# Layer 0's router input: transposing six of eight batches with VectorE blocks and a DRAM round trip instead of TensorE

## The chip, the cores and the metric

The kernel runs on one core of a Trainium2 chip. The metric is the device time of one execution in microseconds. Before the change the median of three runs is 2222.36 us (2220.96 to 2223.24). The profile is of one execution more, which took 2228.55 us. Engines are named as the profile names them: PE is TensorE (PEld its weight loads), DVE is VectorE, ACT is ScalarE, POOL is GpSimd, and SP issues most DMA transfers.

## The reference

Input x has 8 batches of 512 tokens with 512 values, all float32. Four stages follow each other, each with a residual and a layernorm:

```python
x = _layernorm(x + _L0_attn_ref(x, ...))   # 16 causal heads of 32
x = _layernorm(x + _L0_ffn_ref(x, ...))    # 8 experts, top 2 per token
x = _layernorm(x + _L1_attn_ref(x, ...))   # 8 query heads of 64, 2 key/value heads
x = _layernorm(x + _L1_ffn_ref(x, ...))    # gated feed-forward, integer weights
```

Only the seam between the first two is touched. The router of the second stage takes the normalised rows of the first and needs, per token, 8 logits, a softmax and the two largest:

```python
router_logits = xf @ gate_weight.T + xf @ gate_delta.T
probs = jax.nn.softmax(router_logits.astype(jnp.float32), axis=-1)
routing_weights, selected = jax.lax.top_k(probs, TOP_K)
```

## The kernel before

The function `attention0` computes the first stage batch by batch (b = 0 to 7). A batch has four groups of four heads (g = 0 to 3), and a group has three units (u = 0 to 2), which split the causal scores by key tile: 512, 384 + 128 and 256 query columns wide. Below, (g, u) names a unit. In every unit TensorE computes the scores `sc` of the unit (L1356), then some extra work that the plan of the batch puts there, and then the product `av` of the unit before with the values (L1380). In unit u = 1 it also forms the row sums `rs` of the group before (`normalise`, L1395). ScalarE turns `sc` into `p` with an exponential (L1360), GpSimd masks `p` (L1365), and VectorE adds up the `p` of a group (L1388), inverts the row sums (L1398, 3.3 us each) and scales `av` into `aoT` (L1399).

The extra work comes from `plan(b)`, which maps each unit to a list of calls:

- `value`, `query`, `key` (L1282 to L1303) make the values of this batch and the queries and keys of the next group. Each is one set of four matmuls into one PSUM tile.
- `project(b-1, t)` (L1305) is the output projection of the batch before, one call for each of the four token tiles. The last one calls `layernorm` (L173), which normalises the rows on VectorE (L185) and stores them to DRAM (`rows`, L188).
- `turn(b-1, c)` (L1315) transposes the normalised rows with four TensorE transposes of 128 x 128 into one PSUM tile, copied to SBUF as `x1T` by VectorE (L194) or ScalarE (L192). Four calls, c = 0 to 3, make the whole `x1T`.
- `score(b-1)` (L1326) multiplies `x1T` with the router's weights into `ps_logits` (L491), copied out by ScalarE (L1330).
- `choose(b-1)` (L1332, L494) sums the logits' parts on TensorE (`ps_r`, L503) and then runs softmax and top 2 as some 26 small VectorE instructions with one ScalarE exponential (L512).
- `dispatch(b-2)` and `enter(b-2)` (L1335, L1345) rank the tokens per expert (`ps_rank`, L547) and enter them in a table: 24 one-hot rows on VectorE (L577 to L579), then 16 matmuls `ps_table` (L588).
- `merge` (L1404) adds one chunk of LoRA weights to each of two experts: two matmuls `ps_lora` into two PSUM tiles (L781), two scaled copies on ScalarE (L792), two additions on GpSimd (L794).

All these PSUM tiles (`ps_v`, `ps_q`, `ps_k`, `ps_o`, `rs`, `ps_x1T`, `ps_logits`, `ps_r`, `ps_rank`, `ps_table`, `ps_lora`) come from one pool with one tag and two buffers, `mm`, used in turn: a third tile waits until the first is copied out. `sc` has a single buffer. Every engine runs its own instructions in order, and the order inside the first seven batches is made by a scheduler from the order of the calls; from the third group of the last batch on it is the written order. SP's queue is one such order too: the `rows` stores (L188), the loads of `xT` (L1244) and of `x` (L1248) stand in it. GpSimd also adds a bias to each batch's `x` (L1474), which needs that load.

A way of transposing without TensorE is already in the kernel, in the class `Turn` (L73 to L102), which the third and the fourth stage use: VectorE transposes 32 x 32 blocks inside each 128 x 512 tile (`blocks`), four DMAs store the result to DRAM so that the blocks fall into their places (`out`, 256 KB each in pieces of 512 bytes), and one DMA of 1 MB loads it back (`back`). The columns of the result stand in another order, which `by_tile` undoes in a later copy:

```python
def blocks(self, room, t, x):
    out = room.rearrange("p (j t c) -> p j t c", t=self.n, c=32)[:, :, t, :]
    self.nc.vector.transpose(out, x.rearrange("p (j c) -> p j c", c=32))

def out(self, room):
    for i in range(self.N):
        src = room[32 * i : 32 * (i + 1), :].rearrange("r (k j f) -> r k j f", j=self.N, f=self.n * 32)
        self.nc.sync.dma_start(out=self.dram.rearrange("(j r) k i f -> r k j i f", j=self.N)[:, :, :, i, :], in_=src)

def back(self, room):
    self.nc.sync.dma_start(out=room, in_=self.dram.rearrange("p k i f -> p (k i f)"))
```

Of the kernel before, what the change touches and what calls it, by code (L numbers as in the profile page):

```python
# [9 lines left out]
F32 = mybir.dt.float32  # L10
# [3 lines left out]
AF = mybir.ActivationFunctionType  # L14
ALU = mybir.AluOpType
# [3 lines left out]
P = 128  # L19
NB = 8  # L20
S = 512
D = 512
NT = S // P
ND = D // P
# [29 lines left out]
V_BQ, V_BK, V_NS, V_SS, V_SG, V_SU = 0, 4, 8, 12, 16, 16 + NHID  # L54
# [18 lines left out]
class Turn:  # L73
# [11 lines left out]
# [4 lines that stand above are left out]
# [662 lines left out]
class Experts:  # L751
# [8 lines left out]
    def room(self, i):  # L760

        at = 4 * EXPERT + i * ND * 512
        return self.w[:, at : at + ND * 512].rearrange("p (u f) -> p u f", f=512)
# [450 lines left out]
def attention0(env, guard, keep, routes, experts, dram, p_mm, tiles_ctx):  # L1214
# [4 lines left out]
    tc, nc, ins, xs, vec = env.tc, env.nc, env.ins, env.xs, env.vec  # L1219
# [3 lines left out]
    with ExitStack() as phase:  # L1223
        work = phase.enter_context(tc.tile_pool(name="a_work", bufs=1))
# [54 lines left out]
        def mm(shape, name):  # L1279
            return p_mm.tile(shape, F32, tag="mm", name=name)  # L1280

        def value(b, t):  # L1282
            ps = mm([P, D], "ps_v")
            for c in range(ND):
                nc.tensor.matmul(ps, lhsT=xts[b][:, c, ts(t, P)], rhs=wv[:, c, :], start=c == 0, stop=c == ND - 1)  # L1285
            vs[t] = own.tile([P, D], F32, tag=f"v{t}", name=f"v{t}")
            nc.vector.tensor_tensor(vs[t], ps, row[:, 0, :], ALU.add)  # L1287

        def query(b, g):
            ps = mm([P, S], "ps_q")  # L1290
            for c in range(ND):
                nc.tensor.matmul(ps, lhsT=wq[:, g, ts(c, P)], rhs=xts[b][:, c, :], start=c == 0, stop=c == ND - 1)  # L1292
            q = own.tile([P, S], F32, tag="q", name="q", bufs=2)
            nc.vector.tensor_scalar(q, ps, vec[:, V_BQ + g : V_BQ + g + 1], None, ALU.add)
            heads[b, g] = [q]

        def key(b, g):
            ps = mm([P, S], "ps_k")
            for c in range(ND):
                nc.tensor.matmul(ps, lhsT=wk[:, g, ts(c, P)], rhs=xts[b][:, c, :], start=c == 0, stop=c == ND - 1)  # L1300
            k = own.tile([P, S], F32, tag="k", name="k", bufs=2)
            nc.scalar.activation(k, ps, AF.Identity, bias=vec[:, V_BK + g : V_BK + g + 1])
            heads[b, g].append(k)  # L1303

        def project(b, t):  # L1305
            ps = mm([P, D], "ps_o")
            for c in range(ND):
                nc.tensor.matmul(ps, lhsT=aoTs[b][:, c, ts(t, P)], rhs=wo[:, c, :], start=c == 0, stop=c == ND - 1)
            nc.vector.tensor_tensor(xs[b][:, t, :], ps, xs[b][:, t, :], ALU.add)
            if t == NT - 1:  # L1310
                env.layernorm(b, router.rows[S * b : S * (b + 1)])

        x1Ts, logits = {}, {}

        def turn(b, c):  # L1315
            if c == 0:
                x1Ts[b] = work.tile([P, ND, S], F32, tag="x1T", name="x1T")
            ps = mm([P, S], "ps_x1T")
            for t in range(NT):
                nc.tensor.transpose(ps[:, ts(t, P)], xs[b][:, t, ts(c, P)], env.ident)  # L1320
            if b == NB - 2:
                nc.scalar.copy(x1Ts[b][:, c, :], ps)
            else:
                env.evacuate(c, x1Ts[b][:, c, :], ps)

        def score(b):  # L1326
            ps = mm([P, S], "ps_logits")
            router.logits(x1Ts.pop(b), ps)
            logits[b] = work.tile([P, S], F32, tag="logits", name="logits")
            nc.scalar.copy(logits[b], ps)  # L1330

        def choose(b):  # L1332
            router.choose(b, logits.pop(b), mm([P, NT, E], "ps_r"))

        def dispatch(b):  # L1335
            router.dispatch(b, mm([P, NT, E], "ps_rank"))
# [3 lines left out]
        def one_hot(b, places):  # L1340
            if places[0] == 0:
                rooms[b] = work.tile([P, ND, S], F32, tag="x1T", name="one_hot")
            return router.one_hot(b, rooms[b], places)

        def enter(rows):  # L1345
            router.enter(mm([P, 2, E * E_TILES], "ps_table"), *rows)

        def scores(b, g, u):
            q, k = heads[b, g]
            sc = p_sc.tile([P, 4, S], F32, tag="sc", name="sc")  # L1350
            width = 0
            for kt in UNITS[u]:
                w = S - P * kt
                for j in range(4):
                    hs = slice(HD * j, HD * (j + 1))
                    nc.tensor.matmul(sc[:, j, width : width + w], lhsT=k[hs, ts(kt, P)], rhs=q[hs, P * kt :],  # L1356
                                     start=True, stop=True)
                width += w
            p = own.tile([P, 4, width], F32, tag=f"p{u}", name="p", bufs=2 if u == 0 else 1)
            nc.scalar.activation(p, sc[:, :, :width], AF.Exp, scale=scale)  # L1360

            at = 0
            for kt in UNITS[u]:
                first = p[:, :, at : at + P]
                nc.gpsimd.affine_select(out=first, in_=first, pattern=[[0, 4], [1, P]], compare_op=ALU.is_ge, fill=0.0,  # L1365
                                        base=0, channel_multiplier=-1)
                at += S - P * kt
            return p
# [41 lines left out]
        def plan(b):  # L1410

            todo = {(g, u): [] for g in range(ND) for u in range(len(UNITS))}
            for slot, places in (((0, 0), (0, 1)), ((0, 1), (3,)), ((0, 2), (2,))):
                todo[slot] += [lambda t=t: value(b, t) for t in places]
            for g in range(ND):
                nb, ng = (b, g + 1) if g + 1 < ND else (b + 1, 0)
                if nb < NB:
                    todo[g, 1].append(lambda nb=nb, ng=ng: query(nb, ng))
                    todo[g, 2].append(lambda nb=nb, ng=ng: key(nb, ng))
            pb, last = b - 1, b == NB - 1  # L1420
            if b:
                places = ((1, 0), (1, 0), (1, 1), (1, 1) if last else (1, 2))
                for t, slot in enumerate(places):
                    todo[slot].append(lambda t=t: project(pb, t))
                places = ((2, 0),) * 4 if last else ((2, 1), (2, 1), (2, 2), (2, 2))
                for c, slot in enumerate(places):
                    todo[slot].append(lambda c=c: turn(pb, c))
                todo[(2, 1) if last else (3, 0)].append(lambda: score(pb))
                todo[(2, 2) if last else (3, 1)].append(lambda: choose(pb))
                if not last:  # L1430
                    todo[2, 0].append(merge)
                    todo[3, 0].append(merge)
            if b == 0:
                todo[1, 0].append(lambda: router.merge_lora(mm([P, ND, E], "ps_wr")))
            if b > 1:
                todo[0, 2].append(lambda: dispatch(b - 2))
                todo[1, 1].append(lambda: enter(one_hot(b - 2, range(NT))))
            if last:
                todo[1, 2].append(soon)
                todo[2, 2].append(first_rows)  # L1440
                todo[3, 1].append(lambda: dispatch(b - 1))
                todo[3, 2].append(begin)
            return todo
# [17 lines left out]
        begun = phase.enter_context(ExitStack())  # L1461
        begun.enter_context(in_order(tc))
        query(0, 0)
        key(0, 0)
        order = phase.enter_context(ExitStack())
        waiting = summing = None
        for b in range(NB):
            todo = plan(b)
            for g in range(ND):
# [16 lines left out]
                for u in range(len(UNITS)):  # L1486
                    p = scores(b, g, u)
# [15 lines left out]
        b = NB - 1  # L1503
# [11 lines left out]
        for c in range(ND):  # L1515
            turn(b, c)
        tiles.step()
        score(b)
        merge()
        choose(b)  # L1520
# [651 lines left out]
```

## Time and profile before

| | us |
|---|---|
| median of three runs | 2222.36 |
| the profiled execution | 2228.55 |
| its span | 2226.8 |
| PE busy in the span | 2191.9 (98%) |
| DVE busy | 1273.7 (57%) |
| ACT busy | 632.0 (28%) |
| POOL busy | 487.6 (22%) |
| `ps_v` of batch 1 starts | 84.25 |
| `ps_v` of batch 7 starts | 644.44 |

The page gives busy times over the whole span, which has stages with different limits. The change lies in the first stage, up to about 745 us, so the views that matter are those of this stretch: the order in time of each engine, and the waits. Two things are to be kept in mind in reading them. The ends of matmuls are modelled, so a wait inside a group of matmuls can be counted as busy; the distance from one group's start to the next is the safer measure. And a group in the order of time is merged: `x4` are four instructions; a float32 matmul of the program shows as two instructions here, a transpose as one.

### The profile page before, as it was taken

To read this page: it belongs to the slowest core of one execution; us is meant where nothing else is said; L and a number is where in the kernel's file an instruction comes from. 1 tells how busy PE (TensorE), PEld (TensorE's weight loads), DVE (VectorE), ACT (ScalarE), POOL (GpSimd) and SP (SyncE) were. 2 spreads that over 40 slices of the span, in tenths; PEclk is the share of its full clock that TensorE was granted. 3 is DMA by queue.
4 is the path that set the end of the run, shared out by engine and by line. 5 is a ranking of instruction groups with operands and counts; after the bars stand their busy time and mean duration, and the time that the engine had idled before them with its cause. 6 is when DMAs were issued, how large, how long until landed. Compare 5 with 4: busy or idle time off the path is not lost. (4 is left out here: it accounts for less than half of the span.)

```text
span 2226.8 us, 23678 instructions
## 1 busy us (share of the span) xinstructions
PE 2191.9 (98%) x9006; PEld 1116.6 (50%) x9006; DVE 1273.7 (57%) x2032; ACT 632.0 (28%) x917; POOL 487.6 (22%) x489
## 2 busy tenths in 40 slices
PE   9999999999999999999999999999999999999997
PEld 3344444444444444444443333333343778888876
DVE  3556666666666633323316887798757655555443
ACT  2332323323233232122124333223332222222222
POOL 2322423234132333122105222222211000000000
PEclk9999999999999899999999999999999999999999
DMA  8010101101022216888735212312110321111000
GB/s 297 20 57 1 57 10 48 58 1 58 5 71 94 85 57 181 227 218 214 191 114 193 80 57 86 95 55 77 45 32 13 109 78 57 57 57 57 20 20 21
DMA packets 146428, 182.20 MB, mean 82 GB/s; under 512 B 60530, under 2 KB 89202, under 8 KB 144514
## 3 DMA queue, kind: packets, MB, share of 16 engines
q1 hardware_dynamic: 135024, 144.91, 21.0%
q0 software_dynamic: 10560, 34.61, 5.5%
q8 instruction: 74, 1.21, 0.2%
q10 hardware_dynamic: 722, 1.07, 0.1%
q14 instruction: 48, 0.39, 0.1%
HBM read 117.38 MB, written 63.18 MB: 81 GB/s over the span
## 5 line engine op out<-in xcount | busy, mean ns | idle before, releaser
L903 PE MATMUL ps_gu<-experts,xrT 128*128 128x512 f32 (+1 forms) x520 | 248.8, 601 | 0.0
L1360 ACT ACTIVATE p<-sc 128x2048 f32<-128x2048 f32 (+1 forms) x96 | 152.8, 1592 | 190.0 <-PE sc L1356 183.1
L1148 DVE SCALAR_TENSOR_TENSOR hT<-ps_u,vec,sg 128x512 f32<-128x512 f32 x88 | 65.6, 745 | 195.2 <-PE ps_u L1143 195.2
L1365 POOL TENSOR_SCALAR_AFFINE_SELECT p<-p 128x512 f32<-128x512 f32 x128 | 91.6, 729 | 385.2 <-ACT p L1360 378.5
L1159 PE MATMUL ps_f<-ffn_w,h_half 128*128 128x512 f32 x672 | 170.2, 394 | 0.6 <-issue 0.4
L998 POOL TENSOR_TENSOR g_total<-g_total,r_inv 128x512 f32<-128x512 f32 x64 | 89.7, 1401 | 358.3 <-DVE r_inv L1735 283.0
L1705 ACT ACTIVATE p<-sc 128x1024 f32<-128x1024 f32 x128 | 124.0, 1021 | 105.9 <-PE sc L1702 100.8
L1735 DVE RECIPROCAL r_inv<-r_inv 128x512 f32<-128x512 f32 x32 | 107.1, 3346 | 78.8 <-ACT r_inv L995 78.8
L1388 DVE TENSOR_TENSOR p<-p 128x1536 f32<-128x1536 f32 (+2 forms) x96 | 129.4, 1348 | 39.2 <-POOL p L1365 22.2
L905 DVE TENSOR_TENSOR h<-ps_gu,h 128x256 f32<-128x256 f32 x67 | 28.4, 424 | 212.8 <-ACT h L904 212.8
L903 PEld LDWEIGHTS ps_gu<-experts,xrT 128*128 128x128 f32 x520 | 96.2, 197 | 89.7 <-issue 89.5
L1159 PEld LDWEIGHTS ps_f<-ffn_w,h_half 128*128 128x128 f32 x672 | 124.4, 188 | 33.0 <-DVE h_half L1154 5.6
L1143 PE MATMUL ps_g<-x_high,ffn_w 128*128 128x512 f32 x352 | 138.9, 395 | 0.8 <-DVE x L1676 0.8
L1143 PE MATMUL ps_g<-x_low,ffn_w 128*128 128x512 f32 x352 | 139.1, 395 | 0.0
L1143 PE MATMUL ps_u<-x_low,ffn_w 128*128 128x512 f32 x352 | 138.8, 394 | 0.0
L1143 PE MATMUL ps_u<-x_high,ffn_w 128*128 128x512 f32 x352 | 138.7, 394 | 0.0
L919 PE MATMUL ps_y<-experts,hT 128*128 128x512 f32 (+1 forms) x272 | 127.9, 593 | 0.5 <-ACT hT L913 0.5
L1702 PE MATMUL sc<-qT,kT 64*128 64x512 f32 x512 | 127.3, 615 | 1.0 <-ACT qT L1609 0.7
L1292 PE MATMUL ps_q<-experts 128*128 128x512 f32 x256 | 121.1, 615 | 4.4 <-DMA experts<-in_xT 4.4
L1724 PE MATMUL av<-p,v 128*64 128x512 f32 x512 | 123.8, 605 | 0.0
L1285 PE MATMUL ps_v<-experts 128*128 128x512 f32 x256 | 118.0, 609 | 3.3 <-DVE v L1287 3.3
L1670 PE MATMUL ps_o<-attn_out,aoT 128*128 128x512 f32 x256 | 117.9, 605 | 0.8 <-ACT r_inv L995 0.8
(262 smaller groups left out, 3438.5 us busy)
## 6 DMA issues: line engine op xcount, KB each, us to landing
results<-y SPq DMA_DIRECT2D x68, 256.0 KB, 2.3
turned<-turned SPq DMA_DIRECT2D x56, 256.0 KB, 4.1
pair<-xrT SPq DMA_DIRECT2D x25, 512.0 KB, 3.4
xrT<-pair SPq DMA_DIRECT2D x100, 128.0 KB, 4.5
x<-in_x SPq DMA_DIRECT2D x8, 1024.0 KB, 7.5
experts<-in_gate_up SPq DMA_DIRECT2D x8, 1024.0 KB, 10.8
rows<-x SPq DMA_DIRECT2D x32, 256.0 KB, 2.0
x<-rows SPq DMA_DIRECT2D x8, 1024.0 KB, 15.5
```

What stands on the lines that cost most here:

```text
L903: nc.tensor.matmul(ps, lhsT=xT[:, c, :], rhs=self.weights(i, c), start=c == 0, stop=c == ND - 1)
L919: self.nc.tensor.matmul(ps, lhsT=hT[:, c, :], rhs=self.weights(i, ND + c), start=c == 0, stop=c == self.NI - 1)
L1143: nc.tensor.matmul(ps, lhsT=w[:, ts(dc, P)], rhs=x[:, dc, :], start=(dc, i) == (0, 0), stop=(dc, i) == (ND - 1, 1))
L1159: self.nc.tensor.matmul(os[t], lhsT=h[:, ts(t, P)], rhs=self.weights(2 * NHID + c), start=(c, i) == (0, 0), stop=(c, i) == (NHID - 1, 1))
L1285: nc.tensor.matmul(ps, lhsT=xts[b][:, c, ts(t, P)], rhs=wv[:, c, :], start=c == 0, stop=c == ND - 1)
L1292: nc.tensor.matmul(ps, lhsT=wq[:, g, ts(c, P)], rhs=xts[b][:, c, :], start=c == 0, stop=c == ND - 1)
L1360: nc.scalar.activation(p, sc[:, :, :width], AF.Exp, scale=scale)
L1388: nc.vector.tensor_tensor(total[:, :, P * kt :], total[:, :, P * kt :], p[:, :, at : at + w], ALU.add)
L1670: nc.tensor.matmul(ps, lhsT=state[b]["aoT"][:, c, ts(t, P)], rhs=w_out[:, c, :], start=c == 0, stop=c == ND - 1)
L1702: nc.tensor.matmul(sc[:, j, :], lhsT=st["kT"][hs, ts(kt, P)], rhs=st["qT"][g][hs, :], start=True, stop=True)
L1705: nc.scalar.activation(p, sc, AF.Exp, scale=scale)
L1724: nc.tensor.matmul(st["av"][HD * j : HD * (j + 1), :], lhsT=st["v"][:, kt, HD * j : HD * (j + 1)], rhs=p[:, j, :], start=kt == 0, stop=kt ...
```

## The change

For batches 0 to 5 (`by_blocks = NB - 2`) the transposes of `turn` are replaced by `blocks(b)`: four VectorE block transposes, four stores, one load, all through `Turn`. Batches 6 and 7 keep `turn`. `score` of these batches moves from the first unit of group 3 into its last, ahead of the key of the next batch, and its copy puts the columns in order; in the last batch it stays in (2, 1), but ahead of the query. `choose` moves into the next batch's first unit, `dispatch` from (0, 2) to (1, 0), and `enter` from (1, 1) to (1, 2). The four `project` calls are spread over four units. In batches 1 to 6 the two `merge` calls move from (2, 0) and (3, 0) to (2, 2) and (3, 1). The query of the next batch moves from (3, 1) to (3, 0). In batches 1 to 6 ScalarE copies out the query of group 3, which VectorE did before.

```diff
             q = own.tile([P, S], F32, tag="q", name="q", bufs=2)
-            nc.vector.tensor_scalar(q, ps, vec[:, V_BQ + g : V_BQ + g + 1], None, ALU.add)
+            if g == ND - 1 and 0 < b <= by_blocks:
+                nc.scalar.activation(q, ps, AF.Identity, bias=vec[:, V_BQ + g : V_BQ + g + 1])
+            else:
+                nc.vector.tensor_scalar(q, ps, vec[:, V_BQ + g : V_BQ + g + 1], None, ALU.add)
...
+        by_blocks = NB - 2
+        turns = Turn(env, dram, NT, "turned0")
+
+        def room(b):
+            x1Ts[b] = work.tile([P, ND, S], F32, tag="x1T", name="x1T")
+
+        def blocks(b):
+            room(b)
+            flat = x1Ts[b].rearrange("p k s -> p (k s)")
+            for t in range(NT):
+                turns.blocks(flat, t, xs[b][:, t, :])
+            turns.out(flat)
+            turns.back(flat)
+
         def turn(b, c):
             if c == 0:
-                x1Ts[b] = work.tile([P, ND, S], F32, tag="x1T", name="x1T")
+                room(b)
...
-            nc.scalar.copy(logits[b], ps)
+            if b < by_blocks:
+                nc.scalar.copy(turns.by_tile(logits[b], False), turns.by_tile(ps, True))
+            else:
+                nc.scalar.copy(logits[b], ps)
...
+            pb, last = b - 1, b == NB - 1
+            by_dma = 0 <= pb < by_blocks
             for g in range(ND):
                 nb, ng = (b, g + 1) if g + 1 < ND else (b + 1, 0)
                 if nb < NB:
-                    todo[g, 1].append(lambda nb=nb, ng=ng: query(nb, ng))
+                    todo[g, 0 if by_dma and ng == 0 else 1].append(lambda nb=nb, ng=ng: query(nb, ng))
                     todo[g, 2].append(lambda nb=nb, ng=ng: key(nb, ng))
-            pb, last = b - 1, b == NB - 1
             if b:
-                places = ((1, 0), (1, 0), (1, 1), (1, 1) if last else (1, 2))
+                places = ((1, 0), (1, 1), (1, 2), (2, 0)) if by_dma else ((1, 0), (1, 0), (1, 1), (1, 1) if last else (1, 2))
                 for t, slot in enumerate(places):
                     todo[slot].append(lambda t=t: project(pb, t))
-                places = ((2, 0),) * 4 if last else ((2, 1), (2, 1), (2, 2), (2, 2))
-                for c, slot in enumerate(places):
-                    todo[slot].append(lambda c=c: turn(pb, c))
-                todo[(2, 1) if last else (3, 0)].append(lambda: score(pb))
-                todo[(2, 2) if last else (3, 1)].append(lambda: choose(pb))
+                if by_dma:
+                    todo[2, 1].append(lambda: blocks(pb))
+                else:
+                    for c in range(ND):
+                        todo[2, 0].append(lambda c=c: turn(pb, c))
+                todo[(3, 2) if by_dma else (2, 1)].insert(0, lambda: score(pb))
+                if not by_dma:
+                    todo[2, 2].append(lambda: choose(pb))
                 if not last:
-                    todo[2, 0].append(merge)
-                    todo[3, 0].append(merge)
+                    todo[2, 2 if by_dma else 1].append(merge)
+                    todo[3, 1].append(merge)
             if b == 0:
                 todo[1, 0].append(lambda: router.merge_lora(mm([P, ND, E], "ps_wr")))
             if b > 1:
-                todo[0, 2].append(lambda: dispatch(b - 2))
-                todo[1, 1].append(lambda: enter(one_hot(b - 2, range(NT))))
+                todo[0, 0].append(lambda: choose(b - 2))
+                todo[1, 0].append(lambda: dispatch(b - 2))
+                todo[1, 2].append(lambda: enter(one_hot(b - 2, range(NT))))
```

As built, the order on SP in batches 1 to 6 becomes: four `rows` stores, four `out` stores, the load of the next `x`, `back`, and in batches 1 to 5 the load of the `xT` of two batches on. On VectorE the four block transposes stand right behind the four instructions of the layernorm (L185), ahead of the next sum of `p` and the next reciprocal.

## Prediction

> **What bounds the kernel now.** I read the page's busy times first, then the table of stretches for the batches of the first stage, then TensorE's order in time within one batch, then its waits, and last the other engines' order in the same batch. The first is the page's line of busy times, the second one batch's stretch (length; busy time of PE, PEld, DVE, ACT, POOL; granted clock; DMA share; GB/s).
>
> ```profile
> PE 2191.9 (98%) x9006; PEld 1116.6 (50%) x9006; DVE 1273.7 (57%) x2032; ACT 632.0 (28%) x917; POOL 487.6 (22%) x489
> ```
> ```profile
> 464.20:557.10 92.90, 92.33 (x477) 39.66 (x476) 59.51 (x106) 28.27 (x32) 28.89 (x27) 1.00 0.10 35
> ```
>
> TensorE is the limit, in the touched stage too. So an edit is worth what it does to TensorE's sequence: work taken out of it, and waits inside it, which the busy share hides because ends are modelled. Batch 5, units (2, 0) to (3, 1), in TensorE's order in time (start, length, line, operation, wait before):
>
> ```profile
> 515.11 1.03 PE L781 MATMUL ps_lora<-lora 16*128 16x512 f32 x4
> 516.06 0.64 PE L1380 MATMUL av<-p,v 128*32 128x256 f32 x8
> 517.27 1.15 PE L1356 MATMUL sc<-q,k 32*128 32x384 f32 x16 [0.57 <-ACT p L1360]
> 518.35 3.70 PE L1292 MATMUL ps_q<-experts 128*128 128x512 f32 x8
> 521.88 0.60 PE L1320 MATMUL ps_x1T<-ident,x 128*128 128x128 f32 x4
> 522.41 1.05 PE L1380 MATMUL av<-p,v 128*32 128x512 f32 x2
> 523.39 0.66 PE L1320 MATMUL ps_x1T<-ident,x 128*128 128x128 f32 x4
> ...
> 525.83 0.71 PE L1356 MATMUL sc<-q,k 32*128 32x256 f32 x8
> 526.47 3.70 PE L1300 MATMUL ps_k<-experts 128*128 128x512 f32 x8
> 530.01 0.60 PE L1320 MATMUL ps_x1T<-ident,x 128*128 128x128 f32 x4
> ...
> 532.88 1.14 PE L1356 MATMUL sc<-q,k 32*128 32x512 f32 x8
> ```
>
> The reader should compare starts. Two `av` matmuls take 0.98 us (522.41 to 523.39), where eight alone take 0.88 (474.05 to 474.93): the next transposes wait for a PSUM tile.
>
> Undisturbed steps, start to start, around this batch: `ps_q`, `ps_k`, `ps_v`, `ps_o` 3.53 each; `sc` 1.07, 1.08, 0.65; `av` 0.88, 1.00, 0.57; `rs` 0.97; a `ps_lora` pair 0.96; `ps_logits` 1.0; `ps_r` 0.89; `ps_rank` 0.45; `ps_table` 1.84. A batch without transposes and waits is 16 x 3.53 + 4 x (2.80 + 2.45 + 0.97) + 2 x 0.96 + 1.0 + 0.89 + 0.45 + 1.84 = 87.5 us (batch 1, which has no `ps_rank` and `ps_table`, 85.2). Batches 1 to 6 take 90.7, 93.5, 96.3, 93.5, 92.9 and 93.3 from `ps_v` to `ps_v`, 560.2 in all, against 522.7 undisturbed: 37.5 us over.
>
> **What the change removes (all on TensorE's path).**
>
> - Transposes: 0.53 + 0.59 + 0.53 + 0.59 = 2.23 us a batch, x 6 = 13.4.
> - Waits among them: 521.88 to 525.83 is 3.95 us, of which `av` and `rs` explain 1.85 and transposes 1.11; 530.01 to 532.88 is 2.87, of which 1.00 and 1.12. Left 0.99 + 0.75 = 1.74 a batch, 10.4.
> - The wait of `sc` for the exponential in (2, 1), where the unit before holds only `merge` and a short `av`: 0.57 a batch, 3.4. `ps_o` now fills that unit.
> - The second `ps_lora` in (3, 0) waits for a tile that ScalarE empties only after an exponential: 532.88 to 538.50 is 5.62 for 4.68 of steps, 0.94 a batch, 5.6.
> - `ps_v` in (0, 1) waits for VectorE, which has `choose` ahead of the two `v` copies. In the changed order the copies come first: 3.3.
>
> The two waits that the view names, between 100 and 640 us (total, times, longest):
>
> ```profile
> PE sc L1356 <- ACT p L1360: 3.4, 6, 0.6
> PE ps_v L1285 <- DVE v L1287: 3.3, 4, 1.7
> ```
>
> Together 36.1; the last 1.4 of the 37.5 I put to one half-clock stretch (granted clock 0.98 in the batch with the 1.7 wait) and don't count.
>
> **What it adds on TensorE's path.** ScalarE's rows:
>
> ```profile
> 515.34 1.88 ACT L1360 ACTIVATE p<-sc 128x2048 f32<-128x2048 f32 x1 [4.85 <-PE sc L1356]
> 517.11 1.08 ACT L792 ACTIVATE scaled<-ps_lora 128x512 f32<-128x512 f32 x2
> 530.21 0.69 ACT L1302 ACTIVATE k<-ps_k,vec 128x512 f32<-128x512 f32 x1 [2.58 <-PE ps_k L1300]
> ```
>
> In (2, 2) the order is now key, `ps_lora`, `ps_lora`: the second needs the key's tile, which is empty 0.2 + 0.69 + about 0.1 after the key's end, where one `ps_lora` takes 0.48: wait 0.5 to 0.55. In (3, 1) the order is `sc`, two `ps_lora`, `av`, `rs`: `rs` needs the first `ps_lora` tile, whose copy stands behind the exponential. The tile is free 0.19 + 1.77 + 0.6 + 0.1 = 2.65 after `sc`, and TensorE arrives after 0.96 + 0.88 = 1.84: wait 0.8. Sum 1.35 a batch, 8.1. Bounds: nothing if the copies run ahead, and 0.94 + 1.77 (the wait of `sc` for `p` at 722.88 in batch 7, the longest of the stage) = 2.7 a batch, 16.3. I take 1.35, worked from the rows themselves.
>
> **What it adds beside TensorE.** VectorE: four block transposes (0.62 each) for two copies of 0.68 and one of 0.75: +0.4 us a batch. The cover is an idle stretch in group 3:
>
> ```profile
> 542.24 0.75 DVE L1294 TENSOR_SCALAR q<-ps_q,vec 128x512 f32<-128x512 f32 x1 [8.69 <-PE ps_q L1292]
> ```
>
> Their place matters more. Clock from the start of `sc` in (2, 0): `ps_o` ends 4.6, its sum and statistics 6.3, GpSimd's rstd +1.48, layernorm 4.14 long to 11.9, transposes to 14.4. Queued behind are the sum of `p` (1.7) and the reciprocal, to 19.5; GpSimd's `g_total` (1.6) waits for that, and behind it stand two LoRA additions (2.8) and the mask (0.65), done 24.6, when TensorE wants the masked `p` of (3, 0) at 25.4. Cover 0.8 us; past that each microsecond costs 6 us.
>
> SP and DMA. The third stage does the same round trip; its rows are VectorE's transposes, SP's four stores and load, and the load's landing:
>
> ```profile
> 1329.79 2.48 DVE L88 STREAM_TRANSPOSE turned<-xn 128x512 f32<-128x512 f32 x4
> ```
> ```profile
> 1332.31 3.23 SPq L93 DMA_DIRECT2D turned<-turned  x4
> 1338.84 0.34 SPq L96 DMA_DIRECT2D hT<-turned  x1
> ```
> ```profile
> DMA to landing us min/median/max: 4.7/4.8/6.5
> ```
>
> From first transpose to landing 13.9 us: 11.9 + 13.9 = 25.8 on the same clock. TensorE comes to `ps_logits` at 28.8 (units of 5.1, 6.5, 6.1, 5.2, 3.9 and 0.65 long, plus the 1.35). Cover 3.0 us. New here is the 1 MB load of the next `x`, issued between stores and `back` on the same queue. At best it fits into the gap in which `back` waits for the stores (cost 0); at worst its whole 5.4 us (an `xT` load's median landing, same size) goes ahead. Two such loads issued 1.8 us apart (530.20 and 531.99, on SP) are both in by 539.5, 3.9 after one alone would be; I take a third of this, 1.3, since `x` goes out 3.3 us ahead of `back`: margin 1.7. `x` itself has the four stores ahead of it (3.2 us of issue), and GpSimd's bias waits for it, as it does today (2.88 before 539.56): landing near 25, where GpSimd arrives at 24.6; the bias (4.5) and two masks then end near 31, and TensorE wants them at 33.7. The next `xT` goes out behind `back`, but isn't needed for a batch: nothing. ScalarE trades two copies of 0.59 for a query of 0.69: less work.
>
> `ps_r` leaves batch 1 and enters batch 7 (0.89 each way). In batch 7 `ps_table` moves to one unit before the transposes that stay there, which then wait about 0.6 for its tile, against 0.44 today. VectorE's one-hot rows (5.1) now stand ahead of a query copy; the tile is free 0.8 before `rs` needs it.
>
> [...] The trace charges TensorE 2.2 us a batch for its transposes plus 1.7 of waits, against 2.5 of block transposes on VectorE. [...]
>
> **Sum.** -36.1 + 8.1 = -28.0. The profiled execution, 2228.55 (span 2226.8 and 1.75 around it), becomes 2200.6; it stands 6.2 over the runs' median, so 2222.36 becomes 2194.4.
>
> **The rivals.**
>
> - *The round trip is late, and the kernel slower.* `ps_logits` waits at the head of TensorE's queue, with the next key, `av` and all else behind it. For it: the cover is small, and the stores are once seen taking 7.6 instead of 6.5 (1749.93 to 1757.53). With 1.1 for that, 5.4 for `x` and 1.7 for the slowest landing, `back` is 5.2 us late, x 6 = 31: 2225. It decides from 4.7 us on. Against: all three at once, six times. Late by 1 to 3 us is likelier: 2200 to 2212.
> - *VectorE and GpSimd become the limit.* Cover 0.8 us; 1 to 2 us over cost 6 to 12: 2200 to 2206. Against: GpSimd is 28.9 of 92.9 us busy.
> - *Only the transposes go.* The waits reappear at other PSUM tiles, there being still two: -13.4, 2209. Against: the order of tiles, gone through above.
>
> **How the numbers follow.** Forecast as summed, 0.66, with its own range 2187 to 2201 (all new waits gone and the half-clock stretch too, to new waits at their bound). Round trip somewhat late 0.12; VectorE or GpSimd 0.09; only the transposes 0.04. Nothing gained, the trip late by about 4.7 us a batch, 0.03; slower, late by more, 0.06. The range of all, 2186 to 2211, leaves out the last two and the tails of the others. A difference under 0.2% (4.4 us) can't be told from none here: faster 0.91, same 0.03, slower 0.06.
>
> **What would show it.** Batches 2 to 6 near 88.8 us from `ps_v` to `ps_v`; 32 `ps_x1T` matmuls instead of 128; no wait of `sc` for `p` in (2, 1); waits of about 0.5 and 0.8 at the second `ps_lora` and at `rs`; `ps_logits` without a wait for DMA. A wait there, or of `av` for GpSimd, over 1 us in each batch makes this wrong, and so would more half-clock stretches (3.4 us each, costing 1.7).

## The result: slower

| | median of runs, us | profiled execution, us | its span, us |
|---|---|---|---|
| before | 2222.80 (2220.96 to 2225.21) | 2228.55 | 2226.8 |
| after | 2239.82 (2238.03 to 2240.99) | 2240.45 | 2238.7 |

The ratio is 1.0071, with a 95% interval of 1.0059 to 1.0083. The forecast was 2194.4 with a range to 2211: the sign is wrong, and the time lies 45 us above the forecast.

The page's line of busy times, and the stretch of batch 5 from `ps_v` to `ps_v` (columns as before):

```profile
PE 2178.1 (97%) x8910; PEld 1101.0 (49%) x8910; DVE 1269.6 (57%) x2038; ACT 629.3 (28%) x911; POOL 497.9 (22%) x489
```
```profile
464.21:559.61 95.40, 90.61 (x465) 37.44 (x461) 59.61 (x112) 27.83 (x31) 30.81 (x27) 0.98 0.18 56
```

TensorE's work did go down: 96 instructions and 13.8 us of busy time fewer. Yet batch 5 takes 95.4 us instead of 92.9, TensorE is idle for 4.8 us of it, where it was for 0.6 before, and the granted clock is 0.98. From `ps_v` to `ps_v`, batches 1 to 6 now take 92.5, 95.3, 96.1, 95.8, 95.4 and 96.0, 571.1 us together against 560.2: 10.9 more, which is nearly the whole difference of the two profiled executions (11.9). By the medians the difference is 17.0 us: the profiled execution of before stands 5.75 above its median, so that the two profiles show less of it. Batch 7 is as it was (107.3 before, 106.9 after, from `ps_v` to the first `ps_o` of its own rows).

TensorE's waits between 100 and 660 us (total, times, longest):

```profile
PE ps_k L1304 <- ACT r_inv L995: 26.2, 6, 4.8
PE rs L1416 <- ACT scaled L792: 4.2, 6, 0.7
```

The two waits of before are gone. The second of the new ones is the wait at `rs` that the prediction put at 0.8. The first is 4.0 to 4.8 us in each of the six batches, and no step of the prediction has it. TensorE's order in the same batch as shown before, from key of (2, 2) on:

```profile
529.91 3.70 PE L1304 MATMUL ps_k<-experts 128*128 128x512 f32 x8
533.54 1.97 PE L781 MATMUL ps_lora<-lora 16*128 16x512 f32 x4
...
542.69 1.03 PE L781 MATMUL ps_lora<-lora 16*128 16x512 f32 x4
543.65 1.06 PE L1401 MATMUL av<-p,v 128*32 128x512 f32 x8
545.40 1.06 PE L1416 MATMUL rs<-p,ones 128*32 128x512 f32 x8 [0.69 <-ACT scaled L792]
546.40 0.71 PE L1377 MATMUL sc<-q,k 32*128 32x256 f32 x8
547.04 1.06 PE L491 MATMUL ps_logits<-x1T,r_wr 128*32 128x512 f32 x8
552.21 5.40 PE L1304 MATMUL ps_k<-experts 128*128 128x512 f32 x8 [4.10 <-ACT r_inv L995]
557.53 1.07 PE L1401 MATMUL av<-p,v 128*32 128x384 f32 x16
```

The last key of the batch, (3, 2), waits 4.10 us. Then it takes 5.32 us from start to start, where the key of (2, 2) takes 3.63. The reason for the wait is on ScalarE:

```profile
544.76 1.08 ACT L792 ACTIVATE scaled<-ps_lora 128x512 f32<-128x512 f32 x2
551.47 0.60 ACT L995 ACTIVATE r_inv<-rs 128x512 f32<-128x512 f32 x1 [5.63 <-POOL experts L794]
```

and behind it on GpSimd:

```profile
540.86 0.64 POOL L1386 TENSOR_SCALAR_AFFINE_SELECT p<-p 128x512 f32<-128x512 f32 x1
542.98 4.55 POOL L1500 TENSOR_TENSOR x<-x,row 128x2048 f32<-128x2048 f32 x1 [1.48 <-DMA x<-in_x]
547.47 1.23 POOL L1386 TENSOR_SCALAR_AFFINE_SELECT p<-p 128x512 f32<-128x512 f32 x2
548.66 3.99 POOL L794 TENSOR_TENSOR experts<-experts,scaled 128x512 f32<-128x512 f32 x2
```

The chain reads from the bottom up. `merge` writes its two scaled LoRA tiles into buffers of the tag `r_inv`, of which there are two (L1429), and the row sums of `normalise` are copied into the same two (L1417). In (3, 1) the merge takes both of them at 544.76. GpSimd gives the first back only after its LoRA addition, and that stands behind the bias of the next `x` (4.55 us) and two masks. So ScalarE, which could copy the row sums from about 546.6 on, does so at 551.47. Until then `rs` holds its PSUM tile, and the next tile but one, `ps_k`, has none.

The clock stands in a table of stretches (length; busy time of PE, PEld, DVE, ACT, POOL; granted clock):

```profile
549.00:551.00 2.00, 0.00 (x0) 0.00 (x0) 1.31 (x1) 0.00 (x0) 2.00 (x1) 1.00 0.00 0
...
553.00:554.00 1.00, 1.00 (x3) 0.48 (x2) 1.00 (x1) 0.54 (x2) 0.64 (x1) 0.50 0.00 0
```

TensorE idles at full clock, and works at half clock right after it. Each of the six waits of 4.0 us and more is followed by one such stretch of 3.41 us, and each of these keys takes 5.29 to 5.33 us. Before, the same part of the run had one.

### The profile page after: what moved, and what is told of

Its sections match the earlier page's. It is cut to its first block, busy times and chain, and to the rows that moved or that the text cites. A ratio compares the mean times of both kernels' runs of the same rounds, so it can differ in the third digit from the quotient of the medians.

```text
span 2238.7 us, 23557 instructions
## 1 busy us (share of the span) xinstructions
PE 2178.1 (97%) x8910; PEld 1101.0 (49%) x8910; DVE 1269.6 (57%) x2038; ACT 629.3 (28%) x911; POOL 497.9 (22%) x489
## 5 line engine op out<-in xcount | busy, mean ns | idle before, releaser
L1304 PE MATMUL ps_k<-experts 128*128 128x512 f32 x256 | 127.6, 645 | 26.2 <-ACT r_inv L995 26.2
L903 PEld LDWEIGHTS ps_gu<-experts,xrT 128*128 128x128 f32 x520 | 96.1, 197 | 89.8 <-issue 89.5
```

The costliest lines, as they stand in the source:

```text
L903: nc.tensor.matmul(ps, lhsT=xT[:, c, :], rhs=self.weights(i, c), start=c == 0, stop=c == ND - 1)
```

## The experiments

Theory A: the whole loss is the wait for the shared buffers and the half clock that it brings; without it the forecast's sum holds. The first four versions set it against B (the stretches at half clock have a cause of their own) and C (the block transposes or the round trip through DRAM make the chain of VectorE and GpSimd late). Every version starts from the kernel after, except before_fused.

| run | median, us | ratio to before, 95% | batches 1 to 6, us |
|---|---|---|---|
| after | 2239.82 | 1.0059 to 1.0083 | 571.1 |
| fused31 | 2195.89 | 0.9857 to 0.9890 | 533.2 |
| no_bias | 2212.77 | 0.9931 to 0.9965 | 544.0 |
| turn_on_pe | 2248.42 | 1.0095 to 1.0129 | 580.1 |
| old_merges | 2222.41 | 0.9984 to 1.0004 | 555.3 |
| own_buffer | 2206.34 | 0.9901 to 0.9934 | 537.2 |
| halves | 2202.60 | 0.9892 to 0.9925 | 536.4 |
| fused31_turn_on_pe | 2244.83 | 1.0070 to 1.0122 | 577.1 |
| half_bias | 2220.82 | 0.9979 to 1.0004 | 552.2 |
| fused31_no_bias | 2198.66 | 0.9872 to 0.9905 | 530.0 |
| fused31_turn_no_bias | 2225.13 | 0.9990 to 1.0009 | 556.0 |
| before_fused | 2220.26 | 0.9978 to 0.9998 | 555.0 |

The last column is the sum from `ps_v` to `ps_v` in the profiled execution (before: 560.2).

**fused31: a merge without the buffers.** In batches 1 to 6 the merge of (3, 1) is one VectorE instruction for each tile, from PSUM straight into the weights.

```diff
+    def merge_fused(self, e, c, ps):
+        for i in range(len(ps)):
+            self.delta(ps[i], e + i, c)
+        for i in range(len(ps)):
+            w = self.chunk(e + i, c)[:, 0, :]
+            self.nc.vector.scalar_tensor_tensor(w, ps[i], LORA_SCALE, w, ALU.mult, ALU.add)
-                    todo[3, 1].append(merge)
+                    todo[3, 1].append(merge_fused if by_dma else merge)
```

> The changed kernel, but in batches 1 to 6 the merge of unit (3, 1) scales and adds on VectorE straight from PSUM (one scalar_tensor_tensor for each of the two tiles), so it takes no `scaled` tile out of the two `r_inv` buffers and nothing waits for GpSimd there. Theory A (the wait of `ps_k` in (3, 2), 26.2 us, comes from the row sums' copy waiting for an `r_inv` buffer that `scaled` holds until GpSimd has added it, and the half clock after each wait, 6 x 1.8 = 10.8 us, comes from the wait): both go, and with them the 4.2 us wait of `rs` for the scaled copy: 2239.8 - 41 = 2199, between 2194 and 2206; no half-clock stretch in the batches. Theory B (the half clock has its own cause, such as the missing transposes): 2239.8 - 30 = 2210, with the six stretches left. Theory C (the block transposes and the layernorm ahead of VectorE's reciprocal make the chain late): 2236 to 2240, the wait stays.

Measured 2195.89, 0.9873 of before, as Theory A has it and not as B or C do. But the edit also takes two copies from ScalarE and two additions from GpSimd's queue; own_buffer, below, leaves them. The profiled execution is the slowest of its four runs (2202.28). The same place of the batch in its profile:

```profile
513.61 1.03 PE L781 MATMUL ps_lora<-lora 16*128 16x512 f32 x4
514.56 1.06 PE L1408 MATMUL av<-p,v 128*32 128x512 f32 x8
515.44 1.04 PE L1423 MATMUL rs<-p,ones 128*32 128x512 f32 x8
516.42 0.71 PE L1384 MATMUL sc<-q,k 32*128 32x256 f32 x8
517.13 1.06 PE L491 MATMUL ps_logits<-x1T,r_wr 128*32 128x512 f32 x8
518.13 3.70 PE L1311 MATMUL ps_k<-experts 128*128 128x512 f32 x8
521.76 1.07 PE L1408 MATMUL av<-p,v 128*32 128x384 f32 x16
```

No wait is left before the key; it takes 3.63 us. The batch takes 88.7 where the prediction looked for "near 88.8". Against after, the six batches are 37.8 us shorter: 26.2 of `ps_k`'s waits, 4.2 of `rs`'s, 6 x 1.70 = 10.2 of half clock, less 2.4 that `ps_logits` now waits for the round trip (two times) and 1.7 for a stretch at half clock behind the longer of these waits; that makes 36.5 of the 37.8. So one such stretch is left in the batches, where Theory A expected none:

```profile
608.08 1.64 PE L491 MATMUL ps_logits<-x1T,r_wr 128*32 128x512 f32 x8 [2.24 <-DMA x1T<-turned]
```

**no_bias: no bias ahead of the additions.** The output lacks the bias of batches 2 to 7.

```diff
-                    nc.gpsimd.tensor_tensor(xs[b], xs[b], row[:, 1:2, :].to_broadcast([P, NT, D]), ALU.add)
+                    if b < 2:
+                        nc.gpsimd.tensor_tensor(xs[b], xs[b], row[:, 1:2, :].to_broadcast([P, NT, D]), ALU.add)
```

> The changed kernel without GpSimd's bias addition (4.5 us each) for batches 2 to 7, so the attention rows of those batches lack the output bias; all else is kept, `scaled` and the row sums still share two buffers. Theory A: the LoRA additions of (3, 1) follow the masks at once and the buffer is free some 4.5 us earlier; the wait of `ps_k` falls from 4.4 us to under 1 in each batch, and the half-clock stretches go with it: 2239.8 - 26.2 - 10.8 + at most 6 = 2203 to 2209. Theory B: 2214, the stretches stay. Theory C: 2236 to 2240.

Measured 2212.77, 27 us less than after and 4 above the expected range. `ps_k` still waits for GpSimd's additions, 1.15 to 1.55 us in each batch, where under 1 was expected:

```profile
PE ps_k L1304 <- ACT r_inv L995: 8.9, 6, 1.5
```

So the bias is 17.3 of the 26.2 us, and none of the six short waits is followed by half clock, which makes the rest of the gain (10.2 of the 27.1 us by which its six batches are shorter).

**own_buffer: another buffer alone.** The buffer of the logits is free in (3, 1), so the first scaled tile goes there instead of into an `r_inv` buffer. No instruction differs from after, and on no engine does the order.

```diff
+        def merge_own():
+            e, c = merges.pop(0)
+            ps = [mm([P, 512], "ps_lora") for _ in range(2)]
+            experts.merge(e, c, ps, [work.tile([P, 512], F32, tag="logits", name="scaled"),
+                                     work.tile([P, 512], F32, tag="r_inv", name="scaled", bufs=2)])
-                    todo[3, 1].append(merge)
+                    todo[3, 1].append(merge_own if by_dma else merge)
```

> The changed kernel, but in batches 1 to 6 the first scaled tile of the merge in (3,1) lies in the buffer of the logits, which is free there, so that the row sums' copy finds a free r_inv buffer. Instructions and their order stay. Theory A1 (the shared r_inv buffers alone make the stall): the 26.2 us of ps_k's waits and the 10.8 us of half clock go, 2239.8 falls to 2203 (2200 to 2208). Rival A2 (GpSimd's queue is late, and the buffer is only where that shows): GpSimd's two additions still end some 4 us after the row sums, the masks of (3,2) stand behind them, and av of (3,2) waits 2.5 to 4 us for masked p instead, with the half clock after it: 2222 to 2236.

Measured 2206.34: A1. This is the run that singles out the shared buffer, since GpSimd has the same instructions in the same order and its two additions take the same 4.0 us. The wait of `ps_k` is gone, and so are all six stretches at half clock, which speaks against B. ScalarE's rows of batch 4, in the place of the two shown above for after:

```profile
433.46 0.60 ACT L995 ACTIVATE r_inv<-rs 128x512 f32<-128x512 f32 x1 [0.75 <-PE rs L1416]
...
439.09 0.59 ACT L1349 COPY logits<-ps_logits 128x512 f32<-128x512 f32 x1 [4.02 <-POOL experts L794]
```

The wait for GpSimd is still there, 4.02 us, but it has moved to the copy of the logits, which TensorE needs much later. What it still costs there is 0.45 to 0.74 us at the next `sc`, whose `k` is copied behind the logits, in four batches, 2.5 us in all. The account closes: the six batches are 33.9 us shorter than in after, and 26.2 of `ps_k`'s waits and 10.2 of half clock, less 2.5, make 33.9. A2 expected `av` to wait for masked `p`; it does not.

**half_bias: half of that bias.**

```diff
+                    n = NT if b < 2 else NT // 2
-                    nc.gpsimd.tensor_tensor(xs[b], xs[b], row[:, 1:2, :].to_broadcast([P, NT, D]), ALU.add)
+                    nc.gpsimd.tensor_tensor(xs[b][:, :n, :], xs[b][:, :n, :], row[:, 1:2, :].to_broadcast([P, n, D]), ALU.add)
```

> The changed kernel, with GpSimd adding the output bias to half of the rows only for batches 2 to 7 (the output lacks the other half), 4.55 us down to 2.3. A1 and A2 both shorten ps_k's wait by 2.3 us, from 4.4 to 2.1 a batch. What it tells is the clock: if a wait of 2 us still brings a stretch at half clock, 1.8 us a batch stay and the time is 2226 (2222 to 2229); if the clock stays up, as after the 1.5 us of the version without the bias, 2215 (2212 to 2219).

Measured 2220.82 (2215.68 to 2227.19), between the two cases and about as wide as both. The wait is 1.55 to 2.61 us, as expected, and the clock does not go by its length alone: after 1.55, 1.93, 2.21 and 2.34 us it stays up and the key takes 3.63; after 2.07 the key takes 5.33, after 2.61 it takes 6.71:

```profile
441.00:443.00 2.00, 1.37 (x2) 0.84 (x3) 1.39 (x1) 1.97 (x4) 1.52 (x2) 0.51 0.00 0
443.00:445.00 2.00, 2.00 (x3) 0.67 (x2) 2.00 (x2) 0.00 (x0) 0.20 (x1) 0.50 0.00 0
445.00:447.00 2.00, 2.00 (x4) 0.76 (x3) 2.00 (x3) 0.00 (x0) 1.58 (x1) 0.50 0.00 0
```

**old_merges: the merges back at (2, 0) and (3, 0).**

```diff
-                    todo[2, 2 if by_dma else 1].append(merge)
-                    todo[3, 1].append(merge)
+                    todo[2, 0].append(merge)
+                    todo[3, 0].append(merge)
```

> The changed kernel with the two merges back in the units (2, 0) and (3, 0), everything else as changed. Theory A: the row sums of (3, 1) again wait about 1.7 us for a buffer, as in the kernel before, and TensorE almost nothing; `rs` doesn't wait for the scaled copy; the second `ps_lora` waits about 0.35 in each of both units: 2239.8 - 37 - 4 - 1 = 2198, up to 2206 if a wait of 1 us is left in (3, 2). Theory C: 2236 to 2240, the place of the merges doesn't matter.

Measured 2222.41, no different from before, 16 us above the range expected: a miss. Three things show in the trace. The buffers collide with the merge at (3, 0) too. GpSimd has these additions right behind the bias there, ahead of the masks, and they take 2.5 us there, as in (3, 0) of before, instead of 4.0, so `ps_k` waits for less long:

```profile
PE ps_k L1304 <- ACT r_inv L995: 6.5, 6, 1.5
```

Second, a merge costs TensorE more there. Set side by side, batch 5 reaches `rs` of (3, 1) 1.8 us later than in fused31: in (3, 0) the two LoRA tiles stand apart and take 1.05 us each, and the `av` that they cut in two takes 1.11 instead of 0.57, while in (3, 1) the pair takes 0.95. The move of the second merge to (3, 1) thus saves TensorE some 1.7 us a batch, and brings the longer stall with it. Batch 4 has the same steps at (3, 0):

```profile
436.87 1.12 PE L781 MATMUL ps_lora<-lora 16*128 16x512 f32 x2
437.92 0.62 PE L1401 MATMUL av<-p,v 128*32 128x256 f32 x2
438.47 1.12 PE L781 MATMUL ps_lora<-lora 16*128 16x512 f32 x2
439.52 0.63 PE L1401 MATMUL av<-p,v 128*32 128x256 f32 x6
440.08 1.95 PE L1377 MATMUL sc<-q,k 32*128 32x384 f32 x16
```
```profile
440.30:443.70 3.40, 3.40 (x28) 1.33 (x28) 0.00 (x0) 1.57 (x1) 2.74 (x1) 0.50 1.01 396
```

Third, the clock is at half from 440.30 to 443.70 in this batch, although TensorE has no wait in the 3.4 us before. So not every such stretch comes from a wait, and for this one Theory B is right; why it came is open.

**turn_on_pe: the transposes left on TensorE.** All moves stay.

```diff
-            if b < by_blocks:
+            if False:
-                    todo[2, 1].append(lambda: blocks(pb))
+                    for c, slot in enumerate(((2, 1), (2, 1), (2, 2), (2, 2))):
+                        todo[slot].append(lambda c=c: turn(pb, c))
```

> The changed kernel with all its moves, but the transposes of batches 0 to 5 stay on TensorE, in (2, 1) and (2, 2) as before the change; no block transposes, no stores, no load back. Theory A: the wait of `ps_k` stays, since GpSimd still has the bias ahead of the LoRA additions, and the transposes come on top: 2239.8 + 13 to 24 = 2253 to 2264. Theory C: the wait goes, 2222 to 2230.

Measured 2248.42, 5 us below the range of A and 18 above that of C, and neither has the waits right: `ps_k` has none, as C said, but `av` waits for masked `p`, 1.4 to 3.3 us in each of the six batches (the view, up to 680 us, has a seventh, short one). So this run decides nothing between A and C; the next ones show why.

```profile
PE av L1401 <- POOL p L1386: 14.4, 7, 3.3
```

**fused31_turn_on_pe** is the same edit on fused31.

> The version with the (3,1) merge on VectorE, with the transposes of batches 0 to 5 left on TensorE (all moves kept). What the block transposes alone are worth where GpSimd is not late: by the sum of the prediction 13.4 us of transposes and up to 10.4 us of waits among them, so 2195.9 + 13.4 to 23.8 = 2209 to 2220. If the transposes cost TensorE nothing that counts (VectorE's block transposes give it back), within 3 us of 2195.9. If av waits for masked p in (3,1) as it did with the merge on GpSimd (2.4 us a batch, half clock after it): 2225 to 2235.

Measured 2244.83, 10 us above the highest case expected and 49 above fused31, which would be twice the transposes' price in the prediction. GpSimd's order shows why this pair does not measure the transposes (fused31_turn_on_pe first, then fused31; L1512 and L1511 are the bias, L1393 the masks, L801 the LoRA additions):

```profile
448.70 2.50 POOL L801 TENSOR_TENSOR experts<-experts,scaled 128x512 f32<-128x512 f32 x2 [3.63 <-ACT scaled L799]
452.25 4.53 POOL L1512 TENSOR_TENSOR x<-x,row 128x2048 f32<-128x2048 f32 x1 [1.05 <-issue]
456.72 1.82 POOL L1393 TENSOR_SCALAR_AFFINE_SELECT p<-p 128x512 f32<-128x512 f32 x3
```
```profile
422.87 0.64 POOL L1393 TENSOR_SCALAR_AFFINE_SELECT p<-p 128x512 f32<-128x512 f32 x1
425.81 4.56 POOL L1511 TENSOR_TENSOR x<-x,row 128x2048 f32<-128x2048 f32 x1 [2.30 <-DMA x<-in_x]
430.33 3.33 POOL L1393 TENSOR_SCALAR_AFFINE_SELECT p<-p 128x512 f32<-128x512 f32 x3
```

In the version without the four stores, the scheduler's order has the bias one place earlier, ahead of the mask that `av` of (3, 0) needs, and turn_on_pe has it there too. Undoing one part moved another engine's queue.

**fused31_no_bias and fused31_turn_no_bias: the transposes where no bias can move.** Both leave out the bias as no_bias does; the second has the transposes on TensorE.

> The version with the (3,1) merge on VectorE, without the output bias that GpSimd adds for batches 2 to 7 (the output lacks it), so that no bias stands ahead of anything. It is the base for the next run. If fused31's 88.7 us a batch hold no wait that goes back to GpSimd: 2195.9 less the two ps_logits waits of its profile, 2193 to 2197. If a part of them does (the masks of (3,2) behind the bias): 2188 to 2193.

> The same without the bias, with the transposes of batches 0 to 5 left on TensorE: what the transposes themselves are worth when the place of the bias in GpSimd's queue can't differ. By the terms of the prediction (13.4 us of transposes, 10.4 us of waits among them) 13 to 24 us above the run without the bias, 2208 to 2218. If the 49 us that the transposes cost with the bias in place were the transposes' own, 2240 to 2246. If they are worth nothing, 2193 to 2197.

Measured 2198.66 and 2225.13, 2 and 7 us above the ranges expected: the transposes with their waits are worth 26.5 us, 26.0 in the six batches of the two profiles, which speaks against C: with their round trip, the block transposes are a gain. The prediction had 23.8. The first run also shows no part of fused31's time that the bias makes: its interval overlaps fused31's. The second stands where before stands (0.9990 to 1.0009): all the other moves together, with the fused merge and without the bias, bring nothing.

**before_fused: VectorE's merge in the kernel before.**

```diff
-                    todo[3, 0].append(merge)
+                    todo[3, 0].append(merge_fused)
```

> The kernel before, with the merge at (3,0) of batches 1 to 6 done by VectorE straight from PSUM, and nothing else: whether that merge alone makes the gain of fused31 (27 us). By the trace of before it takes the second LoRA tile's wait behind the logits away, 0.9 us a batch at most: 2217 (2215 to 2223). If the merge through ScalarE and GpSimd was what cost before too: 2196 to 2205.

Measured 2220.26 (0.9978 to 0.9998). So fused31's 27 us are not the fused merge's own doing: it gives 4 here, and in the changed kernel it takes a stall away. The 4 us did not come as expected, though: from `sc` of (3, 0) to the next query batch 5 still takes 5.61 us, as in before, so the second LoRA tile waits as long. What its profile lacks are before's waits of `ps_v` (3.3) and the one stretch at half clock.

**halves: one tile at a time.** The two merges of a batch are cut into four, at (2, 0) and (2, 2) through ScalarE and GpSimd, at (3, 0) and (3, 1) by VectorE.

```diff
-                    todo[2, 2 if by_dma else 1].append(merge)
-                    todo[3, 1].append(merge)
+                    for slot, by_vector in (((2, 0), False), ((2, 2), False), ((3, 0), True), ((3, 1), True)):
+                        todo[slot].append(lambda by_vector=by_vector: merge_half(by_vector))
```

> The changed kernel, but the two merges of each of batches 1 to 6 are done one tile at a time, in (2,0) and (2,2) by ScalarE and GpSimd, in (3,0) and (3,1) by one VectorE instruction straight from PSUM. Both A1 and A2 take away the stall here, and a single LoRA tile never waits for a second PSUM tile: 0.95 us a batch less than the version with one merge on VectorE (2195.9), 2190 (2187 to 2195). If one tile at a time makes TensorE wait as long, only in more places: 2195 to 2202. If the extra VectorE instruction in (3,0) delays the rows' transfer, ps_logits waits 1 to 2 us a batch: 2197 to 2205.

Measured 2202.60, 7 above fused31 and not 6 below, although no wait of TensorE is left in batches 1 to 6. The place of the loss is the LoRA tile itself, here in (3, 0) of halves:

```profile
517.79 1.12 PE L781 MATMUL ps_lora<-lora 16*128 16x512 f32 x2
```

One tile takes 1.05 us start to start here and in two more places, and 0.95 in (3, 1); the pair in (3, 1) of fused31, above, takes 0.95 together. By these durations a pair of LoRA tiles takes TensorE no longer than one tile alone, so that four single ones cost 4.1 us a batch and the two pairs of fused31 2.85 (the one in (2, 2) 1.90, its second tile waiting for the key's). The difference x 6 is 7.5 us.

## Why the prediction was wrong

**The step that failed** is "wait 0.8 at `rs` in (3, 1) ... Sum 1.35 a batch, 8.1", with its bounds of nothing to 2.7 a batch. It follows which PSUM tile each step needs, and holds for that: `rs` waits 0.69. But it stops there. It does not follow the two SBUF buffers of tag `r_inv`, which the merge and the row sums share, and so it does not ask when GpSimd gives them back. What stands in its place is 4.37 us of `ps_k`'s wait, 0.69 of `rs`'s, and 1.70 of half clock a batch; the first and the last of these the sum has at nothing.

The numbers for it stood in the prediction's own working. It has GpSimd's bias and two masks "end near 31" on the clock of the trip, which is right: on the same clock, in batch 4, the bias runs from 26.0 to 30.5 and the masks end at 31.7. It compares that with the masked `p` that TensorE wants, and not with what stands next in GpSimd's queue, the LoRA additions, nor with who waits for those.

The other terms, one by one:

- *Transposes and the waits among them, 23.8.* Measured 26.5 by fused31_turn_no_bias against fused31_no_bias. Right, and a little small.
- *The waits of `sc` (3.4) and `ps_v` (3.3).* Gone in after, as said.
- *The second `ps_lora`: 5.6 gone, 0.5 to 0.55 a batch new in (2, 2).* Mis-sized: the pair in (2, 2) takes 1.90 against 0.95, so that the wait is 0.95 a batch and gives all of the 5.6 back, 2.4 more than the sum has.
- *The round trip.* After has no wait of `ps_logits` for DMA. Its stores and loads land 3.2 to 7.9 us after their issue, and fused31, without the stall, waits for it twice, 2.4 us in all, 2.24 of them in one batch. So the margin of 1.7 us was thin, and one batch in six overran it. This rival was the one on the slower side, and it is not what happened.
- *VectorE and GpSimd as the limit.* Not in after, whose `av` does not wait for GpSimd; but GpSimd is the engine behind the stall, and in turn_on_pe, with the bias one place earlier, `av` waits for it. The two LoRA additions, put at 2.8 from a row of before, take 3.5 in (2, 2) and 4.0 in (3, 1) of after.
- *Half clock.* Named as what would make the prediction wrong, at 1.7 us each. It came, six times, as a consequence of the wait: in own_buffer, without the wait, it does not.
- *TensorE's 2.2 us a batch plus 1.7 of waits, against 2.5 on VectorE.* The pair without the bias shows what the exchange is worth: 26.5 us with the transposes off TensorE.
- *The forecast's own range, 2187 to 2201.* It does not come out of the terms: 37.5 and 36.1 - 16.3 = 19.8 from 2222.36 make 2184.9 and 2202.6. Nothing rests on the difference.

How good the rest of the sum was shows in own_buffer, which takes away the stall and nothing else. Its six batches take 537.2 us, where the forecast has 560.2 - 28.0 = 532.2: 5.0 over, of which 2.5 are the waits of `sc` for `k` and 2.4 the mis-sized second `ps_lora`. Its median, 2206.34, is 12 above the forecast of 2194.4. Part of that may be the step from the profile to the runs: the terms were read in an execution 6.2 us above the median and then taken off the median. That fused31 measures 2195.89, so close to 2194.4, is partly luck: it has no wait at `rs`, for which the forecast had counted 4.8. It beats both kernels, by 1.3% and 2.0%.

## What to carry to other kernels

When work is moved to another place in the order, follow every buffer that it takes, SBUF tags as much as PSUM tiles: who else uses the tag, which engine gives it back, and what stands ahead of that in its queue. A tag may be shared harmlessly in one order and stall the limiting engine in the next, with no instruction changed (own_buffer against after, 33 us). And an experiment that undoes one part has to be looked at in all queues, since a scheduler may move another part with it.

## What the runs showed of the hardware

- A wait of TensorE can cost more than its length. After all six waits of 4.0 to 4.8 us (after) the clock went to half for 3.41 us, 1.70 us more for the work in it; after eleven waits of 1.05 to 1.55 us (no_bias, old_merges) never; in between it varied: two times in five after 1.93 to 2.61 us (half_bias), four in six after 1.40 to 3.27 (fused31_turn_on_pe), six in six after 1.39 to 3.28 (turn_on_pe). The length of the wait alone does not decide it: in half_bias the clock stayed up after 2.21 and 2.34 us and went to half after 2.07, and in old_merges it was at half from 440.30 with no wait in the 3.4 us before. In after, the six stretches start 95.57 us apart, all of them, which is 28 times the 3.413 us of one, although the waits start 95.3 to 96.1 apart. What decides was not shown.
- Two LoRA matmuls with 16 rows each took as long as one: 0.95 us for two tiles in (3, 1) of fused31, 0.95 for one in (3, 1) of halves and 1.05 elsewhere in it. Why was not tried.
- GpSimd's two LoRA additions took 3.99 us in (3, 1) of after and 2.50 in (3, 0) of before. Why was not tried.
